# Layer 0's sums of a two-layer convolution kernel: the order in which they are written, and the layout of what is computed from them

## The chip, the cores and the metric

The kernel runs on one core of one Trainium2 chip. Its engines work side by side, each through its own queue of instructions: TensorE (PE; its weight loads are shown as PEld), VectorE (DVE), ScalarE (ACT), GpSimd (POOL) and SyncE (SP), which here only issues DMAs. On-chip memory is SBUF (128 partitions); matmul results lie in PSUM. The metric is the device time of one execution in microseconds. Three runs of the kernel before took 3092.81 to 3095.0 us, median 3093.68.

## The reference

The input `x` is [4, 16, 256, 256] in float32. Two layers are computed, each as `x = x + layer(_gn(x))`, where `_gn` normalizes groups of two channels. The change lies in layer 0, a convolution whose 400 outputs a pixel are weights (25 for each of 16 channels) of that pixel's own 5x5 neighbourhood:

```python
out = conv(x, conv_w, padding='SAME') + conv_b          # 3x3, 16 -> 16 * 25 channels
logits = out.reshape(N, C, K * K, H, W)                 # K = 5
weights = softmax(logits, axis=2)
return einsum('ncuij,ncuij->ncij', _unfold(x), weights) # 5x5 patches of x
```

So each output value is a quotient: the sum of exp(logit) times patch over 25 places, divided by the sum of exp(logit) over the same 25. Layer 1 (a SiLU and a B-spline convolution) isn't touched.

## The kernel before

Layer 0 puts the 128 rows of half an image on the partitions and walks along the columns. A strip is one image half by `SW` = 32 columns; there are 4 images x 2 halves x 8 strips = 64 strips, and each has 8 steps of `JG` = 4 columns. One step does the following:

- PE: for each of four columns a matmul at L791 (in two passes) and one at L795 make 400 logits in PSUM (`lg`, three buffers of two columns each).
- ACT: two instructions at L814 write exp of the logits to the first half of `e`, an SBUF tile of 2 x 4 x 5 x 16 x 5 values a partition (kind, column, row of the patch, channel, column of the patch). `e` has `LAG + 3` = 4 buffers.
- POOL: L819 multiplies them with the patches of x (`u`) into the second half of `e`.
- DVE: L691, the sums, adds up the 25 places of both halves in one `tensor_reduce`: 3200 values in, 2 x 4 x 16 = 128 out, for denominator and numerator, four columns, 16 channels. The results go to `nd`, a tile of a strip (three buffers). `waiting` keeps the sums `LAG` = 1 step behind the products.

When a strip's last sum is made, the rest follows some steps later, put off by `after(k, ...)`, a list of work due in k steps:

- `seed`: ACT takes Ln of the denominators and Exp of its negative (L704, L705): an approximate reciprocal `r`, in PSUM.
- `divide`, two steps on: DVE's L709 and L710 make Newton's step on `r`, which leaves the negative reciprocal; L713 multiplies the numerators with it and writes the product to `o`.
- `apply`, five steps on: POOL's L719 subtracts that from the tile `xc` of x, which lies as [channel, 128 columns]. After every fourth strip `xc` holds 128 finished columns; ACT's L731 takes their statistics for layer 1, and ACT's queue issues the store.

`nd` lies as [kind, column, channel], the order in which the sums come out. `xc` needs [channel, column]. L713 does the turn: it reads along `nd` and writes `o` with an inner step of 32 values (128 bytes).

While layer 0 works on image b, `normalize` prepares image b + 1 in small pieces between the steps: ACT scales, PE transposes, DVE's L366 makes a low part, once a strip on average, and SP stores. For the last image there is nothing to prepare; there `scales` (L182 to L212) makes the first constants of layer 1 instead, in small pieces on DVE, PE, ACT and POOL.

The order on each engine is the order of the program's text: `in_order` ties each instruction to the one before it on its engine. Layer 0 exists twice, as a version without and one with a shift of the logits (arm "g"); a bound on the logits, computed at the start, picks the one without. Layer 1's tiles lie over the memory that layer 0 leaves.

Of the kernel before, what the change touches and what calls it, by code (L numbers as in the profile page):

```python
# [11 lines left out]
F32 = mybir.dt.float32  # L12
# [21 lines left out]
def conv_preact_kernel(  # L34
# [12 lines left out]
    nc = tc.nc  # L47
    B, C, H, W = x.shape
    G = 8
    GC = C // G  # L50
    P = 128
# [8 lines left out]
    SW = 32  # L60
# [4 lines left out]
    JG = 4  # L65
    LAG = 1
# [58 lines left out]
    for r in range(RT):  # L125
        p = SROWS.index(r + 1) * C
# [273 lines left out]
    with tc.tile_pool(name="prep0", bufs=2) as prep, tc.tile_pool(  # L400
        name="pre", bufs=1
    ) as pre, tc.tile_pool(
        name="xin", bufs=3
    ) as xin, tc.tile_pool(name="stat", bufs=2) as stat, tc.tile_pool(
        name="pstat", bufs=1, space=PSUM
# [19 lines left out]
        for dj in range(3):  # L425
            v = conv_wt[dj].rearrange("(d c) n -> c d n", d=3)
# [5 lines left out]
        v = conv_wt[2, 2 * C : 3 * C]  # L432
# [10 lines left out]
        for d in range(3):  # L443
# [3 lines left out]
            v = spl_s[dc]  # L447
# [74 lines left out]
        for b in range(B):  # L522
            st = stat.tile([P, G, NH * (GC if b == 0 else 1), 6], F32, name=f"st0_{b}", tag=f"st0{min(b, 1)}")
            for hf in range(NH):
                n = b * NH + hf
                t = loaded.pop(0)
# [33 lines left out]
            v = hm[:, b * NH : (b + 1) * NH]  # L560
# [50 lines left out]
    def layer0(shift):  # L611

        arm = "g" if shift else ""
        marks = {}
        first = len(nc.cur_bb.bb.instructions)
        with tc.tile_pool(name=f"prep{arm}", bufs=2) as prep, tc.tile_pool(
            name=f"im{arm}", bufs=NIM
        ) as imp, tc.tile_pool(name=f"l0{arm}", bufs=2) as l0, tc.tile_pool(
            name=f"nd{arm}", bufs=3
        ) as ndp, tc.tile_pool(name=f"x1{arm}", bufs=3) as x1p, tc.tile_pool(name=f"ptr{arm}", bufs=1, space=PSUM) as ptr, tc.tile_pool(  # L620
            name=f"plog{arm}", bufs=3, space=PSUM
# [44 lines left out]
            def load_xc(n):  # L666
                b, hf, s = strips[n]
                xc = x1p.tile([P, C, CX], F32, name=f"xc_{n}{arm}", tag="xc")
                nc.sync.dma_start(
                    xc, x[b, :, hf * P : (hf + 1) * P, s * SW : s * SW + CX].rearrange(  # L670
                        "c p w -> p c w")
                )
                return xc
# [5 lines left out]
            def after(k, f, *args):  # L679

                later.append([k, partial(f, *args)])
# [7 lines left out]
            def sums():  # L689
                nd, j, e, done = waiting.pop(0)  # L690
                nc.vector.tensor_reduce(  # L691
                    nd[:, :, j : j + JG, :], e.rearrange("p t j m c d -> p t j c m d"),
                    AX.XY, ALU.add,
                )
                if done is not None:
                    done()

            def finish(n, nd, xc):
                after(LAG + 2, seed, n, nd, xc)


            def seed(n, nd, xc):
                r = prc.tile([P, SW, C], F32, name=f"r_{n}{arm}", tag="r")
                nc.scalar.activation(r, nd[:, 0], AF.Ln)  # L704
                nc.scalar.activation(r, r, AF.Exp, scale=-1.0)  # L705
                after(1, divide, n, nd, xc, r)

            def divide(n, nd, xc, r):
                nc.vector.tensor_mul(nd[:, 0], nd[:, 0], r)  # L709
                nc.vector.scalar_tensor_tensor(r, nd[:, 0], 2.0, r, ALU.subtract, ALU.mult)  # L710

                o = ndp.tile([P, C, SW], F32, name=f"o_{n}{arm}", tag="o", bufs=2)
                nc.vector.tensor_mul(o.rearrange("p c j -> p j c"), nd[:, 1], r)  # L713
                after(LAG + 3, apply, n, o, xc)

            def apply(n, o, xc):
                w0 = strips[n][2] * SW % CX
                v = xc[:, :, w0 : w0 + SW]
                nc.gpsimd.tensor_sub(v, v, o)  # L719
                if w0 + SW == CX:  # L720
                    for g in range(G):
                        after(1 + g, statistics, n, xc, g)
                    after(2, store, n, xc)
# [12 lines left out]
            def store(n, xc):  # L736
# [8 lines left out]
                    name=nc.get_next_instruction_name(), engine=mybir.EngineType.Activation,  # L745
# [8 lines left out]
            nxc, xc = load_xc(0), None  # L754
            ahead = iter(())
            for n, (b, hf, s) in enumerate(strips):
# [12 lines left out]
                if s * SW % CX == 0:  # L769
                    xc = nxc  # L770

                nd = ndp.tile([P, 2, SW, C], F32, name=f"nd_{n}{arm}", tag="nd")
                for j in range(0, SW, JG):
                    if j % CI == 0:
                        k = n * nci + j // CI
# [10 lines left out]
                    e = l0.tile([P, 2, JG, K, C, K], F32, name=f"e_{n}_{j}{arm}", tag="e", bufs=LAG + 3)  # L786
                    for j1 in range(0, JG, 2):
                        lg = plog.tile([P, 2, 512], F32, name=f"lg_{n}_{j}_{j1}{arm}", tag="lg")
                        for i in range(2):
                            o = (j + j1 + i) % CI * RP  # L790
# [9 lines left out]
                        if shift:  # L800
                            mx = l0.tile([P, 2, C], F32, name=f"mx_{n}_{j}_{j1}{arm}", tag="mx")
                            for i in range(2):
                                v = lg[:, i, :NL].rearrange("p (m c d) -> p m c d", m=K, c=C)
# [21 lines left out]
                    if len(waiting) > LAG:  # L825
                        sums()
# [8 lines left out]
            while waiting:  # L835
                sums()
# [224 lines left out]
    with tc.If(fast > 0) as small_logits:  # L1061
        layer1("", *layer0(False))
    with small_logits.Else():
        layer1("g", *layer0(True))
# [42 lines left out]
```

## Time and profile before

| | |
|---|---|
| median of three runs | 3093.68 us (3092.81 to 3095.0) |
| the profiled execution: its own time / its span | 3092.67 / 3090.9 us |
| granted TensorE clock | 0.970 |
| layer 0, first matmul to last instruction of DVE | about 125 to 2073 us |
| the sums, L691 | 512 instructions, mean 3476 ns |
| L709, L710, L713 | 64 each, mean 681, 696 and 1083 ns |
| POOL's product, L819, and its subtraction, L719 | 512 and 64, mean 3547 and 1328 ns |
| exp, L814 | 1024, mean 837 ns |

All tables below come from one profiled execution; times in them are counted from the start of its span. An instruction's record can overlap the start of the next one on the same engine: 3476 ns is how long a sum is in the engine, and from the start of one to the start of the next it is less. On an engine that is never idle the second figure decides.

### The profile page before, as it was taken

The page shows a single profiled execution, that of the slowest core. Times are in us where ns is not written, and L with a number is a line of the kernel's source. Part 1 is how long each engine was busy: PE and PEld are TensorE (multiplying, and loading weights), DVE is VectorE, ACT ScalarE, POOL GpSimd, SP SyncE. Part 2 cuts the span into 40 slices and gives each one's busy share as a digit, 9 for nine tenths or more (in the row PEclk, how much of TensorE's full clock was granted, in tenths as well). Part 3 has the DMA queues.
Part 4 walks back from the last instruction along what each step waited for, and adds up shares of the span by engine and source line. Part 5 has one row for each costly group of instructions (what it writes and reads, how often), then busy time and mean ns, then how long its engine had stood idle before and what let it go on. Part 6 is the DMA issues. An engine that isn't in the chain of part 4 may idle for free.

```text
span 3090.9 us, 40797 instructions
## 1 busy us (share of the span) xinstructions
PE 2840.5 (92%) x14760; PEld 1484.6 (48%) x14760; DVE 2976.4 (96%) x1571; ACT 2240.5 (72%) x2619; POOL 1951.1 (63%) x734
## 2 busy tenths in 40 slices
PE   4499999989999999999999999957999999999998
PEld 3366656656556666666666566632222222222222
DVE  7499999999999999999999999988999999999997
ACT  6466665676766566756646546559999999999995
POOL 4199999999999999999999999970100100000000
PEclk7699999999999999999999999988999999999999
DMA  9988977879878778878867667649999988999994
GB/s 275 284 222 224 249 203 206 219 189 255 230 206 240 191 202 224 242 214 218 221 161 199 164 171 193 156 110 201 194 193 197 197 194 191 197 196 198 193 198 89
DMA packets 352725, 626.36 MB, mean 203 GB/s; under 512 B 41330, under 2 KB 218724, under 8 KB 336644
## 3 DMA queue, kind: packets, MB, share of 16 engines
q1 hardware_dynamic: 318020, 605.29, 79.0%
q10 hardware_dynamic: 33024, 16.78, 1.9%
q8 instruction: 121, 1.98, 0.3%
q0 software_dynamic: 1472, 1.59, 0.2%
q14 instruction: 88, 0.72, 0.1%
HBM read 513.95 MB, written 104.24 MB: 200 GB/s over the span
## 4 chain that ended last, share of the span: by engine, by line
DVE 65%; PE 9%; ACT 9%; issue 8%; DMA 6%; SPq 2%; POOL 1%; DVEq 0%; ACTq 0%; POOLq 0%
DVE nd L691 45%; PE yp L988 3%; PE lg L791 3%; DVE ta L169 3%; DVE ta L168 3%; DVE tb L169 3%; DVE tb L168 3%; DMA sx<-x1s 2%; DVE ring L170 2%; DVE o L713 1%; DVE tb L159 1%; DVE r L710 1%; DMA an<-hsl 1%; ACT sl L924 1%; ACT ta L167 1%
## 5 line engine op out<-in xcount | busy, mean ns | idle before, releaser
L791 PE MATMUL lg<-wm,am 128*128 128x400 f32 x4096 | 1741.2, 506 | 102.9 <-ACT e L814 64.2
L819 POOL TENSOR_TENSOR e<-e,u 128x1600 f32<-128x1600 f32 x512 | 1789.9, 3547 | 67.7 <-ACT e L814 48.6
L691 DVE TENSOR_REDUCE nd<-e 128x128 f32<-128x3200 f32 x512 | 1746.9, 3476 | 31.6 <-POOL e L819 31.5
L795 PE MATMUL lg<-wn,an 97*128 97x400 f32 x2048 | 1349.7, 659 | 12.1 <-DMA an<-hsl 11.9
L814 ACT ACTIVATE e<-lg 128x800 f32<-128x800 f32 x1024 | 817.8, 837 | 726.4 <-DVE nd L691 522.3
L791 PEld LDWEIGHTS lg<-wm,am 128*128 128x128 f32 x4096 | 764.3, 193 | 424.1 <-ACT e L814 113.3
L988 PE MATMUL yp<-ring,wt 128*32 128x512 f32 x6144 | 739.7, 595 | 66.8 <-POOL ring L959 46.5
L795 PEld LDWEIGHTS lg<-wn,an 97*128 97x128 f32 x2048 | 389.3, 190 | 330.3 <-issue 21.1
L988 PEld LDWEIGHTS yp<-ring,wt 128*32 128x32 f32 x6144 | 206.9, 109 | 591.5 <-issue 470.0
L905 POOL MEMSET sx<- 16x256 f32 x8 | 2.4, 302 | 667.2 <-PE yp L996 232.5
L1004 PE MATMUL yp<-sl,ws 64*32 64x512 f32 x1536 | 176.5, 588 | 0.0
L731 ACT ACTIVATE z<-xc,nrm 128x256 f32<-128x256 f32 x256 | 153.6, 600 | 10.5 <-POOL xc L719 6.2
L170 DVE SCALAR_TENSOR_TENSOR ring<-ta,ta 128x2048 f32<-128x2048 f32 (+1 forms) x64 | 147.8, 2309 | 10.8 <-ACT z L731 8.3
L169 DVE TENSOR_TENSOR ta<-ta,ta 128x2048 f32<-128x2048 f32 (+1 forms) x64 | 148.4, 2318 | 2.9 <-ACT ta L167 2.9
L170 DVE SCALAR_TENSOR_TENSOR ring<-tb,tb 128x2048 f32<-128x2048 f32 x64 | 145.6, 2276 | 2.6
L169 DVE TENSOR_TENSOR tb<-tb,tb 128x2048 f32<-128x2048 f32 x64 | 145.2, 2268 | 0.7 <-ACT tb L167 0.7
L924 ACT ACTIVATE sl<-sx,q 64x2048 f32<-64x2048 f32 x64 | 133.4, 2085 | 1.5 <-DMA sx<-x1s 1.4
L194 POOL TENSOR_TENSOR d<-d,nrz 128x8 f32<-128x8 f32 x4 | 2.7, 663 | 200.1 <-DVE d L192 200.1
L167 ACT ACTIVATE ta<-ta 128x2048 f32<-128x2048 f32 (+1 forms) x64 | 123.2, 1925 | 2.0
L167 ACT ACTIVATE tb<-tb 128x2048 f32<-128x2048 f32 x64 | 120.5, 1883 | 0.0
L1004 PEld LDWEIGHTS yp<-sl,ws 64*32 64x32 f32 x1536 | 48.8, 106 | 116.2 <-issue 115.9
L719 POOL TENSOR_TENSOR xc<-xc,o 128x512 f32<-128x512 f32 x64 | 85.0, 1328 | 13.4 <-DVE o L713 13.4
(181 smaller groups left out, 2054.3 us busy)
## 6 DMA issues: line engine op xcount, KB each, us to landing
am<-hst SPq DMA_DIRECT2D x512, 194.6 KB
u<-hs SPq DMA_DIRECT2D x320, 288.0 KB
an<-hsl SPq DMA_DIRECT2D x512, 129.8 KB
xta<-x1s SPq DMA_DIRECT2D x40, 1024.0 KB
xtb<-x1s SPq DMA_DIRECT2D x40, 1024.0 KB
xtc<-x1s SPq DMA_DIRECT2D x40, 1024.0 KB
am<-hst SPq DMA_DIRECT2D x256, 129.8 KB
sx<-x1s SPq DMA_DIRECT2D x248, 128.0 KB
```

The costliest lines, as they stand in the source:

```text
L167: nc.scalar.activation(s1, r1, AF.Square, scale=2.0)
L168: nc.vector.scalar_tensor_tensor(s2, t, 2.0, s2, ALU.subtract, ALU.mult)
L169: nc.vector.tensor_mul(s1, s1, r1)
L170: nc.vector.scalar_tensor_tensor(f, s2, 0.0, s1, ALU.min, ALU.subtract if given else ALU.add)
L691: nc.vector.tensor_reduce(nd[:, :, j : j + JG, :], e.rearrange("p t j m c d -> p t j c m d"), AX.XY, ALU.add,)
L791: nc.tensor.matmul(lg[:, i, :NL], lhsT=am[:, o : o + P], rhs=wm.rearrange("p m c d -> p (m c d)"), start=True, stop=False,)
L795: nc.tensor.matmul(lg[:, i, :NL], lhsT=an[:, o : o + P], rhs=wn.rearrange("p m c d -> p (m c d)"), start=False, stop=True,)
L814: nc.scalar.activation(ev, lg[:, :, :NL], AF.Exp)
L819: nc.gpsimd.tensor_tensor(e[:, 1].rearrange("p j m c d -> p j (m c) d"), e[:, 0].rearrange("p j m c d -> p j (m c) d"), uv, ALU.mult,)
L924: nc.scalar.activation(sl[n % 2][:, :, 1 : W + 1], t, AF.Silu, scale=sc[b][0][0 : RD * C], bias=sc[b][1][0 : RD * C],)
L988: nc.tensor.matmul(yp[t * M : (t + 1) * M], lhsT=wt[:, d, e].rearrange("p r o -> p (r o)"), rhs=ring[:, r0 + t * RT + d : r0 + t * RT + d ...
L1004: nc.tensor.matmul(yp[t * M : (t + 1) * M], lhsT=ws[:, e].rearrange("p r o -> p (r o)"), rhs=sl[n % 2][:, t : t + NT + 1 : NT, e : e + W], ...
```

## The change

The sums write their 128 results in the order of `xc` themselves: `nd` becomes [kind, channel, column], and each `tensor_reduce` writes column by column and channel by channel as before, but to addresses 32 values apart. `r` has the same new layout. Ln, Exp, L709 and L710 run over the same elements, in the order of memory. The last product is made in place in the second half of `nd`, with no turn, and POOL subtracts it from there; `o` is gone. A strip's `nd` is thereby held until POOL's subtraction.

```diff
             def sums():
                 nd, j, e, done = waiting.pop(0)
                 nc.vector.tensor_reduce(
-                    nd[:, :, j : j + JG, :], e.rearrange("p t j m c d -> p t j c m d"),
+                    nd[:, :, :, j : j + JG].rearrange("p t c j -> p t j c"),
+                    e.rearrange("p t j m c d -> p t j c m d"),
                     AX.XY, ALU.add,
                 )
...
             def seed(n, nd, xc):
-                r = prc.tile([P, SW, C], F32, name=f"r_{n}{arm}", tag="r")
+                r = prc.tile([P, C, SW], F32, name=f"r_{n}{arm}", tag="r")
                 nc.scalar.activation(r, nd[:, 0], AF.Ln)
                 nc.scalar.activation(r, r, AF.Exp, scale=-1.0)
                 after(1, divide, n, nd, xc, r)
 
             def divide(n, nd, xc, r):
                 nc.vector.tensor_mul(nd[:, 0], nd[:, 0], r)
                 nc.vector.scalar_tensor_tensor(r, nd[:, 0], 2.0, r, ALU.subtract, ALU.mult)
-
-                o = ndp.tile([P, C, SW], F32, name=f"o_{n}{arm}", tag="o", bufs=2)
-                nc.vector.tensor_mul(o.rearrange("p c j -> p j c"), nd[:, 1], r)
-                after(LAG + 3, apply, n, o, xc)
-
-            def apply(n, o, xc):
+                nc.vector.tensor_mul(nd[:, 1], nd[:, 1], r)
+                after(LAG + 3, apply, n, nd, xc)
+
+            def apply(n, nd, xc):
                 w0 = strips[n][2] * SW % CX
                 v = xc[:, :, w0 : w0 + SW]
-                nc.gpsimd.tensor_sub(v, v, o)
+                nc.gpsimd.tensor_sub(v, v, nd[:, 1])
...
-                nd = ndp.tile([P, 2, SW, C], F32, name=f"nd_{n}{arm}", tag="nd")
+                nd = ndp.tile([P, 2, C, SW], F32, name=f"nd_{n}{arm}", tag="nd")
```

In the changed kernel the sums stand at L691 still, Ln and Exp at L705 and L706, Newton's step at L710 and L711, the last product at L712 and POOL's subtraction at L718.

## The prediction

> **What bounds the kernel now.** I read the page's busy table first, then its slices, then the busy time by window, then who waited for whom in layer 0, and last VectorE's own timeline. In the page, DVE leads and most of the chain of work that ended last is one line, the sums of layer 0:
>
> ```profile
> PE 2840.5 (92%) x14760; PEld 1484.6 (48%) x14760; DVE 2976.4 (96%) x1571; ACT 2240.5 (72%) x2619; POOL 1951.1 (63%) x734
> DVE nd L691 45%; PE yp L988 3%; PE lg L791 3%; DVE ta L169 3%; DVE ta L168 3%; DVE tb L169 3%; DVE tb L168 3%; DMA sx<-x1s 2%; DVE ring L170 2%; DVE o L713 1%; DVE tb L159 1%; DVE r L710 1%; DMA an<-hsl 1%; ACT sl L924 1%; ACT ta L167 1%
> ```
>
> POOL's 63% is an average over two stages. Layer 0 lasts from about 125 to 2073 us (first and last work on its tiles), and by window (columns: window, its length, then PE, PEld, DVE, ACT and POOL busy with counts, clock, DMA share, GB/s) its steady part reads:
>
> ```profile
> 200.00:2060.00 1860.00, 1760.15 (x6131) 1133.64 (x6129) 1853.52 (x749) 1155.21 (x1967) 1812.79 (x570) 0.99 0.77 206
> ```
>
> DVE is busy 99.7% there, POOL 97.5%, PE 94.6%. Three engines stand close together, so busy time alone doesn't say which is the bound. The waits in the same window do:
>
> ```profile
> ACT e L814 <- DVE nd L691: 522.3, 325, 4.8
> DVE nd L691 <- POOL e L819: 2.1, 3, 1.2
> ```
>
> ACT stands 522.3 us waiting for DVE to free an `e` buffer; DVE waits 2.1 us for POOL. DVE is the bound and the rest is held back by its buffers. What it does in a strip, in order of time (start, length, group; from the last quarter, where no other work is mixed in):
>
> ```profile
> 1791.70 27.21 DVE L691 TENSOR_REDUCE nd<-e 128x128 f32<-128x3200 f32 x8
> 1818.82 0.69 DVE L709 TENSOR_TENSOR nd<-nd,r 128x512 f32<-128x512 f32 x1
> 1819.54 0.70 DVE L710 SCALAR_TENSOR_TENSOR r<-nd,r 128x512 f32<-128x512 f32 x1
> 1820.27 1.07 DVE L713 TENSOR_TENSOR o<-nd,r 128x512 f32<-128x512 f32 x1
> 1821.17 27.22 DVE L691 TENSOR_REDUCE nd<-e 128x128 f32<-128x3200 f32 x8
> 1848.30 0.68 DVE L709 TENSOR_TENSOR nd<-nd,r 128x512 f32<-128x512 f32 x1
> ```
>
> A strip takes 1848.30 - 1818.82 = 29.48 us: eight sums in 27.12 (3.39 from start to start), and 0.72 + 0.73 + 0.90 for the three small ones. L709 and L713 have the same operands (SBUF times PSUM, 512 elements) and differ only in how the result is laid down, contiguous or every 128 bytes:
>
> ```profile
> L709 DVE TENSOR_TENSOR nd<-nd,r x64: 667/679/699, 193.6 to 2070.8; 128x512 f32<-128x512 f32 x64
> L713 DVE TENSOR_TENSOR o<-nd,r x64: 1022/1082/1110, 195.1 to 2072.2; 128x512 f32<-128x512 f32 x64
> ```
>
> [...] 1082 - 679 = 403 ns over 512 elements, 0.79 ns for each scattered write[...] L709 to L713 each read one SBUF and one PSUM tensor, and POOL's product keeps to 3503 to 3637 ns throughout.[...]
>
> **The change part by part.**
>
> *Newton's last product.* L713 now writes in place, contiguously. Its nearest rows are L709 (the same operands and form, also in place, 679) and L366 (PSUM minus SBUF to contiguous SBUF, 681). What counts on a saturated engine is start to next start. L713 held the engine for 0.90 to 0.95 us, mean about 0.92 (in the timeline around 1010 us: 1011.39 to 1012.31, 1041.49 to 1042.41). L366, which like L713 is followed by an instruction independent of it, holds it for 0.60 (1012.31 to 1012.91). Saving 0.32 us a strip, 64 x 0.32 = 20.5 us. Bounds: by record lengths 0.403 x 64 = 25.8; at least the 0.72 that L709 takes before a dependent successor, 0.20 x 64 = 12.8. I take 20.5.
>
> *The sums.* 512 instructions read what they read before and write 128 values with an inner step of 128 bytes instead of contiguously. Nothing in the trace of before is a sum with scattered results. From above: each of 128 writes pays L713's 0.79 ns, 101 ns a sum, 51.5 us in all. From below: zero; a gain is excluded, since the output was contiguous and the pace is the reading. A result leaves only every 25 elements (3200/128), some 26 ns, and L713 shows that scattered writes can be drained every 1082/512 = 2.1 ns. I take zero; a longer tail of the record itself (up to 0.1 us) would overlap the next sum, as L713's 1.08 us record overlapped its successor by 0.16.[...]
>
> *Seed and denominators.* Ln, Exp and L709, L710 run over the same 512 elements contiguously, in another order: nothing. POOL's subtraction reads a contiguous [16, 32] block as before: nothing.
>
> *Lifetimes.* `o` disappears, and `nd` is held until POOL's subtraction, five steps past its last reader before. It has three buffers; the strip that reuses it starts seven steps after that subtraction, and its first sum waits for a POOL product that stands behind the subtraction on POOL. The program of the chosen branch has the same waits on DVE, ACT, PE and SP as before. No price. Memory gets 4 KB a partition shorter in front of `xc`; in layer 1 POOL's copy of `pad` no longer waits for ACT, and the next POOL copy does: at 2087 to 2093 us, with POOL idle before and after it. Zero.
>
> *What is late next.* POOL without waits needs 29.08 us a strip (subtractions at 1806.29, 1835.37, 1864.45), against DVE's 29.48 - 0.32 = 29.16 in the last quarter, where there is no L366. In the three quarters before, one L366 a strip makes DVE 30.1 - 0.32 = 29.8. PE at its best runs a step in 4 x 0.86 = 3.44, 27.5 a strip before transposes. So DVE stays the bound, by 0.7 us a strip in three quarters and by 0.08 in the last. There, layer 1's scales cost POOL 2 x 2.7 us (1735.65 to 1756.30); DVE starved for 0.40 at 1782.02 already, and with the margin down from 0.40 to 0.08 over about two strips it will starve for about 0.40 + 2 x 0.32 = 1.0. I take 1.5 with the loss of lead after it. Net: 20.5 - 1.5 = 19 us. The very last L713 stands in front of layer 0's end (POOL's subtraction, statistics, store), so its saving counts too.
>
> **The rivals.**
>
> A, the forecast: 3090.9 - 19 = 3071.9 of span; the profiled execution took 3092.67, so 3073.7, and it lay 1.0 below the median of 3093.68, so 3074.7.
>
> B, another engine takes over earlier: POOL's product or ACT's bursts starve DVE once its slack shrinks. For it: POOL at 97.5%, and 0.08 us of margin in the last quarter. Against: DVE waited 2.1 us in 1860. If the last quarter gained nothing and the others half, 48 x 0.16 = 8 us: 3086.
>
> C, slower: the sums pay for every scattered write. 51.5 - 20.5 = 31 us more: 3125. It decides from 20.5/512 = 40 ns a sum, that is from 0.31 ns a write. For it: L713's own price. Against: the 26 ns between writes[...].
>
> D, the change doesn't do what it says: L713's time was not the scatter, the new one takes as long, and nothing moves: 3093. Against it stands L709.
>
> **How the numbers follow.** A 0.80, B 0.07, C 0.09, D 0.04. About 0.2%, 6 us, is what can be told from no change here. Faster by more than that: A and B, 0.87; the same: 0.04; slower: 0.09. The range goes from 3066 (record lengths, 25.8 saved, and a little more) to 3087, which takes in B and the bound of 12.8 us less starvation.
>
> **What would show it.** L691's start-to-start stays 3.39 us; the new L712 is some 680 ns and its successor starts 0.60 after it; a strip of the last quarter takes 29.1 to 29.2; DVE's waits for POOL grow to a few us, all after 1740; layer 1 takes as long as before. L691 at 3.43 or more from start to start would prove me wrong towards C; a POOL without gaps in the first three quarters, towards B.

## The result, and the profile after

The changed kernel takes 3075.21 us (median of 4 runs, 3074.25 to 3078.09) against 3093.24 for the kernel before (3092.17 to 3095.0): ratio 0.9943, 95% interval 0.9925 to 0.996, some 18 us less. The profiled execution has a span of 3076.3 us. It is the slowest of the four: the spans of the other three are 3072.5, 3072.9 and 3073.9, so this trace carries some 2 to 4 us that the others don't have.

The waits of VectorE and ACT in the steady part of layer 0 (200 to 2060 us of the changed kernel; engine and line, what it waited for, us in total, times, longest):

```profile
ACT e L813 <- DVE nd L691: 487.6, 323, 4.4
...
DVE nd L691 <- POOL e L818: 6.5, 7, 1.6
DVE nd L710 <- ACT r L706: 3.2, 1, 3.2
```

ACT still stands waiting for VectorE to free `e`, now 487.6 us instead of 522.3. VectorE remains the bound, with its waits for POOL at 6.5 us in this trace, where they were 2.1; the wait at L710 is the last strip's own, at the end of layer 0, which now lies inside this window. A strip of the last quarter, from VectorE's timeline:

```profile
1808.05 0.68 DVE L710 TENSOR_TENSOR nd<-nd,r 128x512 f32<-128x512 f32 x1
1808.76 0.69 DVE L711 SCALAR_TENSOR_TENSOR r<-nd,r 128x512 f32<-128x512 f32 x1
1809.49 0.69 DVE L712 TENSOR_TENSOR nd<-nd,r 128x512 f32<-128x512 f32 x1
1810.10 27.23 DVE L691 TENSOR_REDUCE nd<-e 128x128 f32<-128x3200 f32 x8
1837.24 0.68 DVE L710 TENSOR_TENSOR nd<-nd,r 128x512 f32<-128x512 f32 x1
```

1837.24 - 1808.05 = 29.19 us, where it was 29.48. The last product holds the engine for 1810.10 - 1809.49 = 0.61, and the eight sums for 27.14, where it was 27.12. The two lines that the change touches, over the whole kernel (duration in ns, minimum, median, maximum):

```profile
L691 DVE TENSOR_REDUCE nd<-e x512: 3473/3477/3492, 136.1 to 2050.7; 128x128 f32<-128x3200 f32 x171
...
L712 DVE TENSOR_TENSOR nd<-nd,r x64: 686/686/690, 195.2 to 2058.8; 128x512 f32<-128x512 f32 x64
```

The sum with scattered results is as long as the one with contiguous results, 3477 against 3476 ns; the last product went from 1082 to 686.

The whole of the difference can be added up from VectorE's records in layer 0, each counted from its start to the next start, idle time over 0.1 us apart. L713's 63 (without the last) held the engine for 58.2 us, L712's 63 hold it for 38.3: 19.9 us less. The sums hold it for 1736.4 instead of 1734.3, 2.1 more, with the same median of 3.393. Idle time between the first and the last sum is 18.5 instead of 14.2, 4.3 more. 19.9 - 2.1 - 4.3 = 13.5, and the last sum starts 13.4 us earlier (2050.7 for 2064.1). The rest of the 14.6 us by which the spans differ is the last L712 and layer 1: 1016.8 us from the end of the last product to the end of the span, 1017.7 before.

So two questions were left: whether those 2.1 us of the sums are the scatter's price, and whether the 4.3 us of waits belong to the change.

### The profile page after: what moved, and what is told of

It reads as the page before. It is cut to its first block, busy times and chain, and to the rows that moved or that the text cites. A ratio compares the mean times of both kernels' runs of the same rounds, so it can differ in the third digit from the quotient of the medians.

```text
span 3076.3 us, 40797 instructions
## 1 busy us (share of the span) xinstructions
PE 2835.5 (92%) x14760; PEld 1479.6 (48%) x14760; DVE 2957.7 (96%) x1571; ACT 2240.5 (73%) x2619; POOL 1952.3 (63%) x734
## 4 chain that ended last, share of the span: by engine, by line
DVE 58%; PE 16%; ACT 9%; issue 7%; DMA 6%; POOL 2%; SPq 2%; DVEq 0%; ACTq 0%; POOLq 0%
DVE nd L691 39%; PE lg L790 9%; PE yp L987 3%; DVE ta L169 3%; DVE tb L169 3%; DVE tb L168 3%; DVE ta L168 3%; PE lg L794 2%; DVE ring L170 2%; DVE tb L159 1%; POOL e L818 1%; ACT ta L167 1%; ACT ta L164 1%; ACT sl L923 1%; ACT ta L166 1%
## 5 line engine op out<-in xcount | busy, mean ns | idle before, releaser
L691 DVE TENSOR_REDUCE nd<-e 128x128 f32<-128x3200 f32 x512 | 1748.8, 3478 | 35.5 <-POOL e L818 35.1
L794 PE MATMUL lg<-wn,an 97*128 97x400 f32 x2048 | 1345.2, 657 | 16.2 <-DMA an<-hsl 16.1
L813 ACT ACTIVATE e<-lg 128x800 f32<-128x800 f32 x1024 | 818.4, 838 | 710.5 <-DVE nd L691 487.6
L170 DVE SCALAR_TENSOR_TENSOR ring<-tb,tb 128x2048 f32<-128x2048 f32 x64 | 145.6, 2276 | 2.6
L718 POOL TENSOR_TENSOR xc<-xc,nd 128x512 f32<-128x512 f32 x64 | 85.7, 1338 | 11.0 <-DVE nd L712 11.0
```

The lines of the kernel that those rows point to most:

```text
L170: nc.vector.scalar_tensor_tensor(f, s2, 0.0, s1, ALU.min, ALU.subtract if given else ALU.add)
L691: nc.vector.tensor_reduce(nd[:, :, :, j : j + JG].rearrange("p t c j -> p t j c"), e.rearrange("p t j m c d -> p t j c m d"), AX.XY, ALU.add,)
L794: nc.tensor.matmul(lg[:, i, :NL], lhsT=an[:, o : o + P], rhs=wn.rearrange("p m c d -> p (m c d)"), start=False, stop=True,)
L813: nc.scalar.activation(ev, lg[:, :, :NL], AF.Exp)
```

## The experiments

### Half and half: the sums alone, the product alone

Scattered sums, and a last product that is scattered as before (the diff is against the changed kernel; inputs are read along memory and the output has an inner step of 128 bytes, as L713 had):

```diff
-                nc.vector.tensor_mul(nd[:, 1], nd[:, 1], r)
-                after(LAG + 3, apply, n, nd, xc)
+                o = ndp.tile([P, C, SW], F32, name=f"o_{n}{arm}", tag="o", bufs=2)
+                turn = o.rearrange("p c j -> p (c j)").rearrange("p (a b) -> p b a", b=SW)
+                nc.vector.tensor_mul(turn, nd[:, 1]..., r...)
+                after(LAG + 3, apply, n, o, xc)
...
-                nc.gpsimd.tensor_sub(v, v, nd[:, 1])
+                nc.gpsimd.tensor_sub(v, v, o)
```

> The sums write every 128 bytes as in the changed kernel, and the last product still writes every 128 bytes too, into o, as before (so the values within a strip lie in another place than x's). If scattered results cost the sums nothing (A), the time is that of the kernel before: ratio 0.999 to 1.001, sums 3.39 us from start to start, 3.48 us long. If each scattered result costs the sums L713's 0.79 ns (C), 51 us more: 1.017, sums 3.49 from start to start. What the changed kernel's trace shows (sums 4 ns longer from start to start on average, with the same median) would be 2 us, 1.0007.

Contiguous sums, and a last product that is contiguous (against the kernel before):

```diff
-                nc.vector.tensor_mul(o.rearrange("p c j -> p j c"), nd[:, 1], r)
+                nc.vector.tensor_mul(o.rearrange("p c j -> p (c j)"),
+                                     nd[:, 1].rearrange("p j c -> p (j c)"),
+                                     r.rearrange("p j c -> p (j c)"))
```

> The sums write contiguously as before; only the last product writes contiguously (its values are then not turned into x's order). A: all of the saving, the product at 0.69 us and 0.60 from start to start, 0.32 x 64 = 20 us less than before, less about 1.5 us of starving in the last quarter: ratio 0.994 as for the changed kernel. C in its small form (scattered sums cost 2 us): 0.9935, that is 2 us less than the changed kernel. If the saving came from the scattered sums in some way instead: 1.000.

The changed kernel once more, beside these two:

> The changed kernel once more, for its time beside the two halves and for a second profile. A: ratio 0.994, span of the profiled execution 3072 to 3077. If the 3 to 4 us of DVE's waits for POOL between 900 and 1420 us that the first profile shows belong to the change (POOL's slack gone), they are there again at the same places; if they are accidents of DMA or of PE, they lie elsewhere or are gone, and the wait of 1.0 us after 1760 us stays.

| kernel | median us | ratio to before | 95% interval |
|---|---|---|---|
| scattered sums only | 3093.0 (13 runs) | 0.9998 | 0.999 to 1.0006 |
| contiguous product only | 3074.14 (5 runs) | 0.9937 | 0.9924 to 0.9951 |
| changed again | 3076.24 (5 runs) | 0.9939 | 0.9925 to 0.9952 |

The lines of the sums and of the last product, first for scattered sums only:

```profile
L691 DVE TENSOR_REDUCE nd<-e x512: 3445/3479/3501, 136.0 to 2068.6; 128x128 f32<-128x3200 f32 x171
...
L714 DVE TENSOR_TENSOR o<-nd,r x64: 1026/1082/1115, 197.0 to 2076.7; 128x512 f32<-128x512 f32 x64
```

and for the contiguous product only:

```profile
L691 DVE TENSOR_REDUCE nd<-e x512: 3470/3476/3487, 136.3 to 2045.9; 128x128 f32<-128x3200 f32 x171
...
L713 DVE TENSOR_TENSOR o<-nd,r x64: 686/686/690, 195.4 to 2054.0; 128x512 f32<-128x512 f32 x64
```

The 1082 ns go with the scattered product and the 686 with the contiguous one, whichever way the sums write; the contiguous product of the second kernel goes to `o`, so writing in place isn't what makes it short. Scattered sums alone cost nothing that can be told: the upper end of the interval, 0.0006 x 3094 = 1.9 us, leaves at most 3.6 ns a sum, where C needed 101 and 40 would have been the point from which it decides. The contiguous product alone brings the whole saving. C is out, and so is D.

The medians of the last two rows differ by 2.1 us, as much as the small form of C expected. Their runs overlap (3072.5 to 3077.89 and 3073.33 to 3076.7), and in the two traces the difference isn't in the sums, which hold VectorE for 1735.8 us in both: it is idle time, 14.1 us for 16.2 between the first and the last sum.

The 2.1 us of the sums aren't the scatter's either. Counted as above, the sums hold VectorE for 1734.5 us when scattered with the old product and for 1735.8 when contiguous with the new one; in the second profile of the changed kernel it is 1735.8. So 1.3 to 1.5 us go with the product, not with how the sums write, and about 1.0 of it lies in one place. The 51 sums that start straight behind a last product take 3376 ns (median) to the next start behind a scattered product, in the kernel before and with scattered sums alone, and 3396 behind a contiguous one: 51 x 0.020 = 1.0 us. Part of what the scattered product seemed to hold the engine for is thus given back by the sum behind it. Why is open. In the first profile another 0.7 us are eight more sums, 24 for 16, that last over 3.41 us to the next start: where VectorE has to wait, the first 84 ns fall under the sum's own record (3477 ns, where the next start comes after 3393) and so aren't counted as idle time.

### The scatter by itself

The price of a scattered result was argued from one pair of lines. 26 extra instructions on VectorE ahead of layer 0, each form twice, measure it (one run, against the changed kernel; `dst` is 512 values, `src` some of the x that is held there):

```diff
+        def every(k):
+            return dst.rearrange("p (a k) -> p k a", k=k)
...
+            nc.vector.tensor_tensor(*product(1))
+            nc.vector.tensor_tensor(*product(2))
...
+            nc.vector.tensor_reduce(*window(1, 1))
+            nc.vector.tensor_reduce(*window(32, 1))
```

> The changed kernel with 26 extra VectorE instructions before layer 0, each on a line of its own, 512 results each: products with an inner step of 4, 8, 16, 32 and 128 bytes, and sums over windows of 1, 2, 4 and 8 values, contiguous and every 128 bytes. If the price is one of how fast results can be put away (A): products 0.68 at 4 bytes and 1.08 at 128; at 16 bytes and above as at 128; a sum over one value pays about 0.4 us when scattered, a sum over two or more nothing (within 0.1 us)[...]. If it is a price for each scattered result (C): 0.4 us more for every window. The time goes up by the probes' 35 to 45 us.

Each line below is one form: L600 to L604 are products whose results lie 4, 8, 16, 32 and 128 bytes apart.

```profile
L600 DVE TENSOR_TENSOR sw<-held x2: 681/683/685, 73.0 to 121.1; 128x512 f32<-128x512 f32 x2
...
L601 DVE TENSOR_TENSOR sw<-held x2: 684/689/694, 73.7 to 122.4; 128x512 f32<-128x512 f32 x2
...
L602 DVE TENSOR_TENSOR sw<-held x2: 1053/1073/1093, 74.4 to 123.2; 128x512 f32<-128x512 f32 x2
...
L603 DVE TENSOR_TENSOR sw<-held x2: 1067/1080/1092, 75.5 to 126.1; 128x512 f32<-128x512 f32 x2
...
L604 DVE TENSOR_TENSOR sw<-held x2: 1026/1044/1062, 76.7 to 127.2; 128x512 f32<-128x512 f32 x2
```

A step of 8 bytes costs nothing that can be told (689 for 683), 16 cost as much as 128. Then the sums, in pairs of contiguous and 128 bytes apart: L611 and L612 over one value, L605 and L606 over two, L607 and L608 over four.

```profile
L611 DVE TENSOR_REDUCE sw<-held x2: 674/680/685, 117.8 to 144.4; 128x512 f32<-128x512 f32 x2
...
L612 DVE TENSOR_REDUCE sw<-held x2: 1015/1016/1018, 118.5 to 145.1; 128x512 f32<-128x512 f32 x2
...
L605 DVE TENSOR_REDUCE sw<-held x2: 1204/1212/1220, 79.5 to 128.3; 128x512 f32<-128x1024 f32 x2
...
L606 DVE TENSOR_REDUCE sw<-held x2: 1197/1206/1214, 86.8 to 129.5; 128x512 f32<-128x1024 f32 x2
...
L607 DVE TENSOR_REDUCE sw<-held x2: 2276/2276/2277, 89.4 to 130.8; 128x512 f32<-128x2048 f32 x2
...
L608 DVE TENSOR_REDUCE sw<-held x2: 2275/2282/2289, 93.1 to 133.1; 128x512 f32<-128x2048 f32 x2
```

A sum over a single value pays 336 ns for 512 scattered results, nearly as much as a product (361 to 397). A sum over two pays nothing, and so do those over four and over eight (4404 contiguous, 4392 scattered). So it isn't a price for each result; it looks like a limit on how fast scattered results can be put away: 512 of them took 1016 ns with one value read for each, and a sum over two takes 1212 when contiguous already. The sums of layer 0 read 25. The forms are two instructions each, but the differences are far above the spread of each. The total time was 3100.7 us in its one run, 25 above the changed kernel and not 35 to 45: the probes' records come to 44 us, but the first sum of layer 0 starts only 27 us later (163.3 for 136.3), so most of the rest must have fallen into time that VectorE spent waiting before.

### Waits for POOL: the change's, or an accident

The second profile of the changed kernel has VectorE's waits for POOL near the same times as the first: 1.1 and 0.5 us between 1110 and 1200, 2.2 and 2.1 between 1380 and 1440, 1.0 and 1.0 between 1750 and 1800. (Before 1110 us they differ, 2.2 and 0.3.) They belong to places in the program, then: near 1170 us it is the fourth sum of the 35th strip that waits, near 1410 us the third and fourth of the 43rd, near 1770 us the fourth of the 55th. Whether they belong to the change is another matter, and the traces of all kernels at the same sums say so (idle time of VectorE before these sums, where it is over 0.1 us; the last column is all of it between the first sum and the last):

| kernel | near 1170 | near 1410 | near 1770 | all |
|---|---|---|---|---|
| before | 0 | 0 | 0.40 | 14.2 |
| scattered sums only | 0 | 1.87 | 0.42 | 18.3 |
| contiguous product only | 0.20 | 0.58 | 0.98 | 14.1 |
| changed | 1.08 | 2.22 | 0.99 | 18.5 |
| changed again | 0.53 | 2.12 | 0.98 | 16.2 |
| changed, with probes | 1.08 | 0 | 0.98 | 14.7 |

The first two rows have the scattered last product, the others the contiguous one. The wait near 1770 us goes with it in every trace, the one near 1170 us too. The one near 1410 us doesn't: it is there with the old product and absent from the changed kernel with probes. From the waits of scattered sums only between 1395 and 1432 us:

```profile
PE lg L792 <- DMA am<-hst: 3.1, 1, 3.1
...
DVE nd L691 <- POOL e L820: 1.9, 2, 1.2
```

And the 4.3 us of idle time that the first profile has more than before are within what two kernels of the same pace differ by, 14.2 and 18.3.

What is late near 1170 and 1410 us is a load: PE waits for `am` in both windows, in the kernel before too (4.8 and 2.2 us). From the waits between 1130 and 1175 us, before:

```profile
PE lg L791 <- DMA am<-hst: 4.8, 1, 4.8
```

and changed:

```profile
PE lg L790 <- DMA am<-hst: 5.1, 1, 5.1
POOL e L818 <- ACT e L813: 4.9, 1, 4.9
...
DVE nd L691 <- POOL e L818: 1.1, 1, 1.1
```

The same load is late by the same 5 us. Before, VectorE saw nothing of it, and neither does it with scattered sums alone, where PE waits 4.7 us. The likely reason is that the products that POOL had ready bridged it, and that VectorE, a little faster now, uses them up sooner and feels the last microsecond. `o`'s memory was put to use against that, with a fourth buffer for `am` and its load one step earlier:

```diff
-                am = imp.tile([P, CI * RP], F32, name=f"am{n}{arm}", tag="am")
+                am = imp.tile([P, CI * RP], F32, name=f"am{n}{arm}", tag="am", bufs=NIM + 1)
...
                         if k + 2 < len(strips) * nci:
-                            ims.append(load_im(k + 2))
-                        am, an = ims.pop(0)
+                            ims.append(load_an(k + 2))
+                        if k + 3 < len(strips) * nci:
+                            ams.append(load_am(k + 3))
+                        am, an = ams.pop(0), ims.pop(0)
```

> The changed kernel with the load of am issued one more step ahead, in a fourth buffer, for which the memory of o makes room (an as before). In the profiles of the changed kernel PE waits 4.5 to 5.1 us for am near 1170 us and 3.3 to 3.6 near 1410, and VectorE then waits 0.5 to 2.2 us for POOL. If these late loads are what is left of VectorE's idle time: 2 to 4 us less than the changed kernel, ratio about 0.993, and no wait of VectorE between 200 and 1700 us. If SP's queue or the DMA engines are simply behind there, nothing changes: 0.994.

It took 3074.55 us, 0.9943 (0.9929 to 0.9956): no gain that can be told from the changed kernel. In its profile VectorE's wait near 1170 us is gone and the one near 1410 is down to 0.7, but the longest idle stretch at the start of layer 0 is 13.3 us, where it was 11.3. From the first sum to the last it takes 1911.5 us, the changed kernel's second profile 1911.7. That one more load stands in front of the first steps may be why the start is longer, but it isn't shown: with scattered sums alone, whose loads are as before, that stretch is 13.0. Nor is the theory of the late load proved. PE no longer waits for `am` in these two windows, but it waits as long for `an`, 4.2 and 5.0 us, whose load was left where it was. What the run does show is that loading `am` earlier brings no time.

### What is next behind VectorE

The prediction put POOL's floor at 29.08 us a strip, 0.1 to 0.7 under VectorE's, and PE's lower still. Three kernels that leave work out test it. Without Newton's step:

```diff
-                nc.vector.tensor_mul(nd[:, 0], nd[:, 0], r)
-                nc.vector.scalar_tensor_tensor(r, nd[:, 0], 2.0, r, ALU.subtract, ALU.mult)
                 nc.vector.tensor_mul(nd[:, 1], nd[:, 1], r)
...
-                nc.gpsimd.tensor_sub(v, v, nd[:, 1])
+                nc.gpsimd.tensor_add(v, v, nd[:, 1])
```

> The changed kernel without Newton's step (L710 and L711 left out; POOL adds instead of subtracts), so the quotient has only the accuracy of Ln and Exp. It takes 0.71 + 0.73 = 1.44 us a strip, 92 us in all, from VectorE and nothing from the others. If VectorE were the bound with much room behind it (B wrong altogether): 3075 - 92 = 2983. If POOL is next, at 29.08 us a strip: 64 x 29.08 + 5.4 for the scales = 1866 us of POOL work, plus some 12 at the start; first to last sum 1875 to 1890 instead of 1912, time 3037 to 3052, with VectorE waiting for POOL in every strip.

Without the subtraction (the line `nc.gpsimd.tensor_sub(v, v, nd[:, 1])` removed), and without both:

> The changed kernel without POOL's subtraction (x is stored as it came, 64 x 1.24 us less POOL work). A: VectorE stays the bound, so only its few waits for POOL go: from the first sum to the last 1912 to 1914 becomes 1907 to 1910; after the last sum a further 4 us or so go, because the statistics no longer wait for the last subtraction. Time about 3065 to 3070. B (POOL as much a bound as VectorE): first to last sum shorter by much more, up to 20 us.

> Both left out. VectorE 28.35 us a strip for three quarters and 27.75 in the last, 1805 in all; POOL 27.84, 1787; PE 27.5 before transposes, 1760 and more. If the three floors are as read from the profile of before: first to last sum 1820 to 1845, 65 to 90 us less than the changed kernel, that is, the two cuts together bring more than the sum of the one (36 at most) and the other (5).

| kernel | median us | ratio to before, interval | first to last sum, us |
|---|---|---|---|
| changed (second profile) | 3076.24 | 0.9939 (0.9925 to 0.9952) | 1911.7 |
| no Newton's step | 3054.23 | 0.9867 (0.9852 to 0.9882) | 1891.6 |
| no subtraction | 3066.27 | 0.9917 (0.9902 to 0.9932) | 1907.0 |
| neither | 3010.1 | 0.9737 (0.9722 to 0.9752) | 1845.4 |

The last column compares best: the first row's medians are of another occasion than the others', on which the kernel before took 3094.07 us and not 3092.59.

Newton's step is 92 us of VectorE's time, and leaving it out brings 20 from the first sum to the last, and about as much of the total. VectorE's waits from 200 to 2000 us, and POOL's timeline, say where the other 70 or so went:

```profile
DVE nd L691 <- POOL e L816: 60.6, 65, 2.6
```

```profile
1835.45 27.94 POOL L816 TENSOR_TENSOR e<-e,u 128x1600 f32<-128x1600 f32 x8
1863.31 1.32 POOL L716 TENSOR_TENSOR xc<-xc,nd 128x512 f32<-128x512 f32 x1
1864.54 27.95 POOL L816 TENSOR_TENSOR e<-e,u 128x1600 f32<-128x1600 f32 x8
1892.40 1.32 POOL L716 TENSOR_TENSOR xc<-xc,nd 128x512 f32<-128x512 f32 x1
```

POOL runs without a gap here, 1892.40 - 1863.31 = 29.09 us a strip, and VectorE now waits for it 65 times; over all of layer 0, 58 of the 64 strips have such a wait. Besides these 60.6 us, the sums hold VectorE for 11 us more than in the changed kernel (1746.9 for 1735.8): a wait counts as idle time only once it has used up the 84 ns by which a sum's record overlaps the next (3477 for 3393). Without the subtraction VectorE has no wait for POOL left after the start of layer 0 (its longest stretches of idle time in layer 0 all lie before 165 us), and the first-to-last time falls by 4.7 us, no more: POOL is not a bound beside VectorE but the one behind it. From first to last sum the two cuts together bring 66 us, where singly they bring 20 and 5. After the last sum about 6 us go, where some 4 were expected: ACT waited 5.8 us there for the last subtraction before it could take the statistics. Without Newton's step the time was expected a little low, 3037 to 3052 for 3054, and 1875 to 1890 us from first to last sum for 1891.6; the forecast took POOL to run without waits, and it waited 14.4 us from 200 to 2000 us, most of it for ACT's exp. Without both, 1845.4 lies just above 1820 to 1845. In that last kernel VectorE still waits 25.6 us for POOL, POOL 35.1 for ACT's exp, and ACT 471.5 for PE's logits, which points at PE as the next in line; no run tests that.

The kernel without Newton's step still writes a quotient, but with only the accuracy of Ln and Exp; it isn't the same computation and isn't offered as a version.

## Why the prediction was right

- *The total.* A saving of 19 us, to 3074.7, was forecast; 3075.21 and, on the second occasion, 3076.24 were measured, 18.0 and 17.8 us below the kernel before.
- *Newton's last product.* 20.5 us were forecast, from L366's 0.60 from start to next start; L712's median is 0.605, and 63 of them save 19.9 us, of which the sums behind them take back 1.0. The bound worked out from record lengths, 25.8, would have been too much: L713's record overlapped its successor by 0.16 us, L712's does by 0.08.
- *The sums.* Zero was taken, between zero and 51.5 us. The sums' records are 3477 ns for 3476, and the scattered sums alone move the time by -0.1 to +0.06%. The reason given, that results leave more slowly than scattered ones can be put away, is what the probes show, and L713's pace was a good measure of it: one result every 2.1 ns was named as what surely passes, and sums over two, which pay nothing, deliver about that: two more values for each of the 512 results took 2276 - 1212 = 1064 ns more, or 2.1 ns a result. The same difference bears out that the sums' pace is the reading, 1.04 ns for each of 1024 values more; by an estimate from it, L691's 3200 values are 3325 of its 3476 ns.
- *What is late next.* VectorE's wait for POOL in the last quarter was forecast at 1.0 us; the five traces with the contiguous product and none of POOL's or VectorE's work left out have 1.0, and both with the scattered one have 0.4. "All after 1740" was wrong: the first profile has 3.3 us of waits between 1110 and 1440, the second 2.6 (none before), behind loads of `am` that are late by 2 to 5 us with and without the change. Only those near 1170 go with the change. Against a term of 1.5 us, idle time between the first and the last sum grew by 4.3 and 2.0 us in the two profiles and not at all with the contiguous product alone; as it differs by 4 us between kernels of the same pace, the traces don't decide whether the term was right. That the total came within 1 us is luck in part: the 95% interval of the measured ratio is some 5 us either way.
- *Lifetimes and layer 1.* Zero was taken. Holding `nd` longer added no wait that the profile shows, and layer 1 takes 1016.8 us for 1017.7. POOL's product has a median of 3540 ns before and after (3503 to 3637, and 3503 to 3677). POOL's copy of `pad` no longer waits for ACT, and the next copy does, as said, with no effect on that time.
- *The rivals.* POOL didn't take over in the changed kernel (B). That it stands right behind VectorE, as the 0.08 us of margin in the last quarter had it, the kernel without Newton's step shows: POOL takes 29.09 us a strip there, VectorE took 29.19. C and D are excluded by the two halves.

## What to carry to other kernels

Where a turn of layout has to be made on VectorE in float32, as here, let an instruction that reads several values for each result make it: there the scattered write was hidden behind the reading (512 results of sums over two, four and eight values took 6 ns less, 6 more and 12 less than contiguous ones; 128 of sums over 25 took 3477 ns for 3476), while an elementwise product of 512 paid 361 to 397 ns for it. Price a saving on a saturated engine from start to next start, not by the length of records (here 19.9 us for 63 products, where record lengths gave 25.8 for 64). And before more is taken from the bound, look how close the next engine stands: here more than three quarters of a further 92 us were lost, most of it to POOL.

## What the hardware showed

A product of 512 float32 values took 683 ns with results 4 bytes apart, 689 at 8, and 1073, 1080 and 1044 at 16, 32 and 128 bytes. Between 8 and 16 bytes it rises by 384 ns, and from 16 to 128 bytes the distance makes little difference; why the step lies there, the runs don't show. What they give is the price of a write on VectorE beyond that step, about 0.76 ns a value by the length of the record ((1073 - 683) / 512) and 0.62 from start to next start (L713's 0.922 us for L712's 0.605), and that it is gone at one result for two values read (1206 ns scattered, 1212 contiguous). One small thing was not expected: a scattered sum over one value pays less (336 ns) than a scattered product (361 to 397), on two samples each. That 128 bytes look a little cheaper than 16 and 32 (1044 for 1073 and 1080) need not mean anything: L713, with the same step in the kernel before, took 1082 in the median of 64.
